# Channel sums of a fused convolution kernel, put off by one tick where a tick has neither a gate nor spectral work

## The chip, the cores and the metric

The kernel runs on one core of a Trainium2 chip. The metric is the device time of one execution in microseconds (us), as the median over several runs. Everything is fp32. The core has a matrix engine (PE, with a second queue PEld for its weight loads), a vector engine (DVE), a scalar engine (ACT), a general engine (POOL) and a queue engine (SP) that here only issues DMAs. PE writes to PSUM alone[...].

## The reference

Two residual layers on `x` of shape (8, 8, 512, 512), each behind a group norm. Cut to what the change touches:

```
# layer 0: x + spectral convolution of _gn(x), a few Fourier modes
# layer 1: x + f(_gn(x)), with f:
grid = drive
for _ in range(15):
    mapped = R * grid * (1.0 - grid)
    local = _conv(mapped, K_local, groups=8)           # 3x3, one filter a channel
    grid = (1 - BETA) * ((1 - EPS) * mapped + EPS * local) + BETA * drive
cml_out = clip(grid, 0.0001, 0.9999)
h = relu(_conv(x, Wp, bp))                             # 3x3, 8 -> 128 channels
nca_out = sigmoid(_conv(h, Wu, bu))                    # 1x1, 128 -> 8 channels
g = sigmoid(_conv(relu(_conv(concat(x, cml_out, nca_out), Wg1, bg1)), Wg2, bg2))
return g * cml_out + (1 - g) * nca_out
```

The 1x1 convolution from the 128 channels of `h` back to 8 is what the kernel calls a channel sum; it is the step that the change moves.

## The kernel before

The eight images ("elements") go through a hand-made schedule of *ticks*. A tick is one call of `work`, and the order in which `work` issues instructions is the order of every engine's queue: `keep_order` pins each engine to the order of the source. An element takes 45 ticks (56 to 415 in the kernel's own count for the eight together); before them stand a prologue with the first element's spectral layer and three ticks of rounds, after them 29 ticks of rounds and gates.

In a full tick the matrix engine gets, in this order:

1. **Three map sets.** A set is a slab of `m` (128 partitions, four rows of 514) that makes one of its 15 steps. `Slabs.convolve` (matmuls at L548) writes 48 products of 32x32 tiles into two of the four PSUM tiles; `settle` drains them with two DVE instructions of 128x1024 (L561), squares each half on ACT (L567), and `renew` swaps border rows with the neighbouring slab by four DMAs from POOL (L594, L595). `settle` is a generator: its first part (both L561, the first squaring) is issued right after the set's matmuls; the second squaring and `renew` come at the next `next(settled)`. For the third set of a tick that is inside the first round, behind the round's ACT instruction.
2. **Up to three rounds.** `Hidden.round` makes four rows of `h`: 12 matmuls at L749 into two PSUM tiles, drained half by ACT (L755) and half by DVE (L757). There are three `h` tiles.
3. **Channel sums** of those rounds. `Hidden.sums` groups the rounds by fours (round number // 4), so that a tick of three rounds has one group or two; `Hidden.point` makes four matmuls a round (L776) into one PSUM bank for each group. The first group of a four is copied to `y` by ACT (L783), a later one added by DVE (L785); when the four are complete ACT takes the sigmoid (L788), and the store of `y` (L791) is put into `rows_due`, which the next tick's `transfers()` empties.
4. **A gate**, where one is loaded (`Gate.conv` L833, `Gate.point` L850), and **spectral pieces** of the next element's layer 0, placed between and beside the channel sums.

In a tick with a gate the gate's matmuls stand between the last round and the sums, or between two groups.

The four PSUM tiles `pair0` to `pair3` are two *halves* of two tiles. `half()` hands them out in turn by the counter `used`: sets of a tick take A, B, A, rounds B, A, B; then the sums use the second tile of a half that the rounds have left (`first[1]`), after `used` has been raised once more:

```
first, second = halves[used[0] % 2], halves[(used[0] + 1) % 2]
if not others.spectral(WIDE, second):
    used[0] += 1
    first, second = second, first
groups = e.hidden.sums()
...
if len(groups) == 2:
    e.hidden.point(groups.pop(0), first[1][:, 0])
...
if groups:
    e.hidden.point(groups[0], first[1][:, 1])
```

The two groups of a tick lie in different banks of the same PSUM tile. In the built program the second group's first matmul nevertheless waits for the DVE addition (L785) that reads the first group's bank.

Map sets go in phases: four sets and then four sets and a tail, 15 steps each, set after set, so that a set comes again four or five places later.

Of the kernel before, what the change touches and what calls it, by code (L numbers as in the profile page):

```python
# [54 lines left out]
TICK = 3  # L55
WIDE, EARLY, FILL, LATE, LAST = "wide", "early", "fill", "late", "last"
# [63 lines left out]
def conv_layers(ctx: ExitStack, tc: tile.TileContext, a, out):  # L120
# [41 lines left out]


    put_off, now, rows_due = [], [0], []
    spare = deque()

    def later(ticks, work):
        put_off.append((now[0] + ticks, work))

    def tick(end=False):  # L170
        now[0] += 1
        due = [w for at, w in put_off if end or at <= now[0]]
        put_off[:] = [] if end else [(at, w) for at, w in put_off if at > now[0]]
        for work in due:
            work()
# [504 lines left out]
    class Phase:  # L680
# [25 lines left out]
        def squares(self, n):  # L706
            while self.squared < len(self.sets) and sets.room():
                if not self.ready(self.squared, 0, n + TICK):
                    break
                self.sets[self.squared].square()  # L710
                self.squared += 1
# [86 lines left out]
    class Gate:  # L798
# [59 lines left out]
        def finish(self):  # L858

            x1, o = (self.mix[: GR * C, q] for q in range(2))  # L860
            nc.vector.scalar_tensor_tensor(  # L861
                o, o, self.e.back[: GR * C, 0:1], x1, ALU.add, ALU.add
            )
            self.store()
# [71 lines left out]
    class Others:  # L936
# [52 lines left out]
        def busy(self):  # L989
            ahead = self.loaded or self.begun  # L990
            return self.before.gates or ahead or self.convolved or self.pointed

        def finish(self):
            while self.pointed:
                self.pointed.popleft().finish()
# [53 lines left out]
    def element(b):  # L1049
        e = Element(b)  # L1050
        phase(e.halves[0])
        phase(e.halves[1] + [e.tail])
        elements.append(e)
        return e

    e = element(0)
# [3 lines left out]
    others = Others()  # L1060
# [24 lines left out]
    halves = pairs[:2], pairs[2:]  # L1085
    used = [0]

    def work(steps, rounds, e, after, gates, transfers, squares=lambda: None):

        double = gates == 2 and not others.lag  # L1090

        def half():
            used[0] += 1
            return halves[used[0] % 2]

        settled = iter(())
        for n, (s, step) in enumerate(steps):
            ps = half()
            s.convolve(step, ps)
            next(settled, None)  # L1100
            if step == 1 and not s.driven:
                s.drive(1)
            settled = s.settle(step, ps)
            next(settled)
            others.finish()
            if gates == 2 and shared.most < 6:
                others.load(1)
                gates = 1
        if steps:
            others.finish()  # L1110
        transfers()
        if steps:
            had = len(others.loaded) + len(others.begun)
            others.load(gates, early=True)
            gates -= len(others.loaded) + len(others.begun) - had
        for _ in range(rounds):
            e.hidden.round(half(), after, settled)
            if spare:
                spare.popleft()()
        next(settled, None)  # L1120
        while spare:
            spare.popleft()()
        others.finish()
        squares()


        first, second = halves[used[0] % 2], halves[(used[0] + 1) % 2]
        if not others.spectral(WIDE, second):
            used[0] += 1
            first, second = second, first  # L1130
        groups = e.hidden.sums()
        gate = others.ready()
        if not gate:
            others.spectral(EARLY, [first[0][:, 0]])
        if len(groups) == 2:
            e.hidden.point(groups.pop(0), first[1][:, 0])
        two = False
        if gate:
            others.conv(first[0][:, 0])
            others.spectral(EARLY, [second[0][:, 0]])  # L1140
            two = others.ready(double)
            if two:
                others.conv(second[0][:, 0])
        if groups:
            e.hidden.point(groups[0], first[1][:, 1])
        others.spectral(FILL, [None])
        others.spectral(LATE, [second[1][:, 0]])
        others.point()
        others.spectral(LAST, [first[1][:, 0]])
        used[0] += two  # L1150
        others.load(gates)
        tick()
        squares()
# [26 lines left out]
    for b in range(B):  # L1180
        e = elements[b]
        after = element(b + 1) if b + 1 < B else None
        others.after = after
        done, rounds = e.hidden.n, ROUNDS if after else ROUNDS_LAST
        first, second = phases[2 * b : 2 * b + 2]
# [98 lines left out]
```

## Time and profile before

| | |
|---|---|
| median of 3 runs | 9116.31 us (9094.66, 9122.18, 9116.31) |
| profiled execution | 9110.93 us, span 9109.1 us, granted clock 0.993 |
| PE busy | 8724.3 us |
| DVE, ACT, POOL busy | 5843.4, 4097.1, 2674.7 us |
| L548 sets, L749 rounds, L776 sums on PE | 3665.0, 2771.8, 998.2 us |
| L833, L850 gates on PE | 951.3, 352.7 us |
| L561 on DVE, one of 128x1024 | 1218 ns |
| L785 on DVE, one of 128x512 | 686 ns (median) |
| L567 / L755 on ACT, one | 1056 / 1114 ns |

The busy time of PE counts matmuls that run beside each other in the array once; a matmul's own 0.6 us is its time through the pipeline, not its price. In lists of waits, "A <- B: total, times, longest" says for how long A's engine stood idle before A and that B's end let it go; "issue" means that nothing in the profile explains the idle time.

### The profile page before, as it was taken

The page shows a single profiled execution, that of the slowest core. Times are in us where ns is not written, and L with a number is a line of the kernel's source. Part 1 is how long each engine was busy: PE and PEld are TensorE (multiplying, and loading weights), DVE is VectorE, ACT ScalarE, POOL GpSimd, SP SyncE. Part 2 cuts the span into 40 slices and gives each one's busy share as a digit, 9 for nine tenths or more (in the row PEclk, how much of TensorE's full clock was granted, in tenths as well). Part 3 has the DMA queues.
Part 4 walks back from the last instruction along what each step waited for, and adds up shares of the span by engine and source line. Part 5 has one row for each costly group of instructions (what it writes and reads, how often), then busy time and mean ns, then how long its engine had stood idle before and what let it go on. Part 6 is the DMA issues. An engine that isn't in the chain of part 4 may idle for free. (4 is left out here: it accounts for less than half of the span.)

```text
span 9109.1 us, 334530 instructions
## 1 busy us (share of the span) xinstructions
PE 8724.3 (96%) x150992; PEld 4143.7 (45%) x150992; DVE 5843.4 (64%) x6304; ACT 4097.1 (45%) x4285; POOL 2674.7 (29%) x4010
## 2 busy tenths in 40 slices
PE   6999999999999999999999999999999999999999
PEld 2445544444444444444444444444444444444433
DVE  6665667656675566765677556775577655666654
ACT  2455445444444444444444444444444444444432
POOL 3222133232323323233232332323323233343323
PEclk9999999999999999999999999999999999999999
DMA  5241356745576555764557645575465754765488
GB/s 165 81 130 40 96 147 167 176 113 147 135 186 165 117 146 145 187 149 116 158 143 193 139 112 157 156 181 136 115 167 149 185 132 110 175 141 142 116 209 204
DMA packets 695970, 1327.26 MB, mean 146 GB/s; under 512 B 147680, under 2 KB 153184, under 8 KB 667056
## 3 DMA queue, kind: packets, MB, share of 16 engines
q1 hardware_dynamic: 587408, 1235.73, 52.9%
q0 software_dynamic: 104992, 69.33, 3.6%
q8 instruction: 1187, 19.45, 0.9%
q14 instruction: 239, 1.96, 0.1%
q10 hardware_dynamic: 2144, 0.80, 0.0%
HBM read 977.48 MB, written 270.61 MB: 137 GB/s over the span
## 5 line engine op out<-in xcount | busy, mean ns | idle before, releaser
L548 PE MATMUL pair<-m,band 32*32 32x512 f32 x103680 | 3665.0, 602 | 151.5 <-issue 125.4
L567 ACT ACTIVATE m<-m 128x1024 f32<-128x1024 f32 x2016 | 2129.1, 1056 | 2044.5 <-DVE m L561 1969.7
L548 PEld LDWEIGHTS pair<-m,band 32*32 32x32 f32 x103680 | 2148.4, 103 | 1601.5 <-issue 790.0
L749 PE MATMUL pair<-cols,w_p 32*128 32x511 f32 (+1 forms) x24576 | 2771.8, 596 | 20.2 <-DMA cols<-xn 12.1
L594 POOL DMA_DIRECT2D m<-m x1568 | 863.4, 551 | 4137.5 <-ACT m L567 4078.9
L749 PEld LDWEIGHTS pair<-cols,w_p 32*128 32x128 f32 x24576 | 1303.3, 185 | 1496.5 <-issue 1164.2
L561 DVE SCALAR_TENSOR_TENSOR m<-pair,dO 128x1024 f32<-128x1024 f32 x1152 | 1355.9, 1218 | 916.8 <-PE pair L548 796.2
L757 DVE TENSOR_SCALAR h<-pair,b_p 128x1024 f32<-128x1024 f32 x1024 | 1313.4, 1283 | 971.5 <-PE pair L749 953.2
L561 DVE SCALAR_TENSOR_TENSOR m<-pair,dE 128x1024 f32<-128x1024 f32 x1008 | 1186.7, 1218 | 845.5 <-PE pair L548 665.7
L755 ACT ACTIVATE h<-pair,b_p 128x1024 f32<-128x1024 f32 x1024 | 1140.1, 1114 | 1176.0 <-PE pair L749 1174.5
L776 PE MATMUL pair<-h,w_u 128*32 128x512 f32 x8192 | 998.2, 596 | 72.4 <-DVE y L785 47.3
L856 POOL TENSOR_TENSOR mix<-mix 96x512 f32<-96x512 f32 x344 | 437.0, 1275 | 1964.4 <-ACT mix L854 1964.3
L833 PE MATMUL pair<-gin,w_g 128*32 128x511 f32 (+1 forms) x8256 | 951.3, 597 | 25.9 <-DMA gin<-nca 15.1
L595 POOL DMA_DIRECT2D m<-m x1568 | 861.0, 549 | 53.8 <-issue 26.4
L833 PEld LDWEIGHTS pair<-gin,w_g 128*32 128x32 f32 x8256 | 252.7, 110 | 674.3 <-issue 602.7
L776 PEld LDWEIGHTS pair<-h,w_u 128*32 128x32 f32 x8192 | 246.4, 109 | 685.8 <-issue 519.4
L788 ACT ACTIVATE y<-y,b_u 128x512 f32<-128x512 f32 x256 | 184.9, 722 | 712.6 <-DVE y L785 712.5
L838 POOL TENSOR_TENSOR mix<-mix 96x512 f32<-96x512 f32 x344 | 444.1, 1294 | 142.4 <-DMA mix<-nca 81.6
L783 ACT COPY y<-pair 128x512 f32<-128x512 f32 x256 | 149.7, 585 | 644.7 <-PE pair L776 626.3
L843 DVE TENSOR_SCALAR mix<-pair,b_g 128x512 f32<-128x512 f32 x344 | 257.0, 747 | 204.2 <-PE pair L833 193.7
L850 PE MATMUL pair<-mix,w_g 128*32 128x512 f32 x2064 | 352.7, 598 | 36.7 <-DVE mix L843 33.1
L839 DVE SCALAR_TENSOR_TENSOR mix<-mix,back 96x512 f32<-96x512 f32 x344 | 311.3, 905 | 30.7 <-DMA mix<-nca 21.3
(96 smaller groups left out, 2612.0 us busy)
## 6 DMA issues: line engine op xcount, KB each, us to landing
gin<-xn SPq DMA_DIRECT2D x344, 384.0 KB
x<-in_x SPq DMA_DIRECT2D x120, 1024.0 KB
cols<-xn SPq DMA_DIRECT2D x240, 512.0 KB
gin<-cml SPq DMA_DIRECT2D x344, 320.0 KB
gin<-nca SPq DMA_DIRECT2D x344, 320.0 KB
dE<-xn SPq DMA_DIRECT2D x288, 256.0 KB
dO<-xn SPq DMA_DIRECT2D x288, 256.0 KB
mix<-xn SPq DMA_DIRECT2D x344, 192.0 KB
```

Source lines behind the costliest of these rows:

```text
L548: nc.tensor.matmul(ps[h // 2][32 * t : 32 * t + 32, h % 2], band[at, self.channel(step - 1, h, t), dx], m[at, t, dx : dx + N], start=(n == ...
L561: nc.vector.scalar_tensor_tensor(u[:, at], ps[q], FLOOR, d[:, at], ALU.max, ALU.add)
L567: nc.scalar.square(u[:, at], u[:, at])
L594: nc.gpsimd.dma_start(out=view(tb, rb, dims), in_=view(ta, ra, dims))
L595: nc.gpsimd.dma_start(out=view(ta, ra + s, dims), in_=view(tb, rb + s, dims))
L749: nc.tensor.matmul(ps[g // 2][:, g % 2, lo:hi], w_p[p, dx, i % 2], self.cols[p, i // 2, at : at + hi - lo], start=(n == 0), stop=(n == 2), ...
L755: nc.scalar.activation(h[:, :2], ps[0], AF.Relu, bias=b_p)
L757: nc.vector.tensor_scalar(h[:, 2:], ps[1], b_p, 0.0, ALU.add, ALU.max)
L776: nc.tensor.matmul(ps[32 * g : 32 * g + 32], w_u[:, r % 4], h[:, g], start=(r == hs[0][0]), stop=(r == hs[-1][0]), tile_position=(0, 32 * g),)
L833: nc.tensor.matmul(ps[32 * j : 32 * j + 32, lo:hi], gband[:, dx], gin[:, j, at : at + hi - lo], start=(n == 0), stop=(n == 2), tile_positi ...
L838: nc.gpsimd.tensor_tensor(d, d, ng, ALU.subtract)
L856: nc.gpsimd.tensor_tensor(d, d, mix[: GR * C, 2], ALU.mult)
```

## The change

A tick counts as *still* when it has three map sets and at least one round, loads no two gates at once, the next element has no spectral piece left (or there is no next element), and no gate is ready at its start. In a still tick the groups of channel sums are not issued; they go to the list `waiting`. The next tick, whatever it is, issues them after its three sets and its `transfers()`, before its rounds. They go into the second tile of the next half in turn, one bank for each group, and `used` is raised by one for them. In a still tick the turn at the end (`used[0] += 1` with the try of a wide spectral piece) is left out.

So around a still tick the halves go: sets A, B, A; the waiting sums B; rounds A, B, A; then the next tick's sets B, A, B. The first round now takes the half of the third set, where before it took that of the second.

```diff
@@ conv_layers
     put_off, now, rows_due = [], [0], []
+    waiting = []
     spare = deque()
@@ class Others
+        def idle(self):
+            return not (self.after and self.after.pieces) and not self.ready()
+
@@ work
+        still = len(steps) == TICK and rounds and not double and others.idle()
         settled = iter(())
         for n, (s, step) in enumerate(steps):
             ps = half()
...
         transfers()
+        for h, hs in waiting:
+            h.point(hs, halves[(used[0] + 1) % 2][1][:, hs[0][0] // 4 % 2])
+        if waiting:
+            used[0] += 1
+        waiting.clear()
         if steps:
             had = len(others.loaded) + len(others.begun)
...
         first, second = halves[used[0] % 2], halves[(used[0] + 1) % 2]
-        if not others.spectral(WIDE, second):
+        if not still and not others.spectral(WIDE, second):
             used[0] += 1
             first, second = second, first
         groups = e.hidden.sums()
         gate = others.ready()
+        if still:
+            waiting.extend((e.hidden, hs) for hs in groups)
+            groups = []
         if not gate:
             others.spectral(EARLY, [first[0][:, 0]])
```

Every instruction of the kernel before is still issued, as often as before; none is new. On POOL the order is the same instruction by instruction. On SP only the stores of `y` (L791) that belong to put-off sums move, one tick later. On DVE and ACT the additions, copies and sigmoids of those sums move from the end of a tick to the place behind the third set's L561 and first L567 of the next tick.

## Prediction

> **What bounds the kernel now.** I read the page first (engine shares, then the groups), then the list of PE's waits, then the timeline of PE and of DVE over three neighbouring ticks, and last the order of the built program's instructions with their waits.
>
> ```profile
> PE 8724.3 (96%) x150992; PEld 4143.7 (45%) x150992; DVE 5843.4 (64%) x6304; ACT 4097.1 (45%) x4285; POOL 2674.7 (29%) x4010
> L776 PE MATMUL pair<-h,w_u 128*32 128x512 f32 x8192 | 998.2, 596 | 72.4 <-DVE y L785 47.3
> ```
>
> PE is busy 96% of the span, so only its remaining 385 us (9109.1 - 8724.3) can be won, and part of that is the start. The change moves L776, before which PE idles 72.4 us in the whole run. PE's waits:
>
> ```profile
> PE pair L548 <- issue: 125.4, 77, 5.5
> PE pair L776 <- DVE y L785: 47.3, 35, 2.3
> ...
> PE pair L776 <- DVE h L757: 16.6, 29, 0.6
> ...
> PE pair L776 <- ACT h L755: 8.5, 19, 1.3
> ```
>
> The largest is idle time before map sets that no wait explains; the change doesn't address it. The three waits of L776 are what it can remove, where they fall into still ticks. Three such ticks of the first element, on PE and then on DVE:
>
> ```profile
> 653.54 9.76 PE L548 MATMUL pair<-m,band 32*32 32x512 f32 x288
> 663.23 8.00 PE L749 MATMUL pair<-cols,w_p 32*128 32x512 f32 x72
> 671.16 1.92 PE L776 MATMUL pair<-h,w_u 128*32 128x512 f32 x16
> 673.98 1.07 PE L776 MATMUL pair<-h,w_u 128*32 128x512 f32 x8 [0.90 <-DVE y L785]
> 674.98 9.76 PE L548 MATMUL pair<-m,band 32*32 32x512 f32 x288
> 684.66 8.00 PE L749 MATMUL pair<-cols,w_p 32*128 32x512 f32 x72
> 692.59 2.78 PE L776 MATMUL pair<-h,w_u 128*32 128x512 f32 x24
> 695.30 9.76 PE L548 MATMUL pair<-m,band 32*32 32x512 f32 x288
> 704.99 5.43 PE L749 MATMUL pair<-cols,w_p 32*128 32x512 f32 x48
> 710.35 1.06 PE L776 MATMUL pair<-h,w_u 128*32 128x512 f32 x8
> 711.68 1.23 PE L776 MATMUL pair<-h,w_u 128*32 128x512 f32 x8 [0.27 <-ACT h L755]
> ```
>
> ```profile
> 660.13 2.36 DVE L561 SCALAR_TENSOR_TENSOR m<-pair,dE 128x1024 f32<-128x1024 f32 x2 [0.76 <-PE pair L548]
> 663.30 2.35 DVE L561 SCALAR_TENSOR_TENSOR m<-pair,dE 128x1024 f32<-128x1024 f32 x2 [0.82 <-PE pair L548]
> 666.18 1.28 DVE L757 TENSOR_SCALAR h<-pair,b_p 128x1024 f32<-128x1024 f32 x1 [0.52 <-PE pair L749]
> ...
> 673.15 0.69 DVE L785 TENSOR_TENSOR y<-y,pair 128x512 f32<-128x512 f32 x1 [0.54 <-PE pair L776]
> ```
>
> Columns are start, duration, instruction, count, and idle time with its releaser. The reader is to see two things. A tick with three rounds and one group has no stall (692.59 follows on 684.66); one with two groups waits 0.90 us for the addition of the first group; one with two rounds waits 0.27 us for the drain of its last round. And DVE begins to drain the third set at 663.30, just as the rounds begin at 663.23: that is the moment into which the change puts the sums.
>
> **What the skill says.** "TensorE: Matmul & The Clock Gate", section "Part 3: Packing small matmuls", has matmuls start and end in strict program order, so that one that waits holds all behind it; the trace agrees (at 711.68 the sets behind are late too). "VectorE: DVE Perf Modes", section "The DRAIN you can't avoid", lets a DVE operation start only when the one before has left the pipe; here two L561 of 1.218 us take 2.35, so an addition behind them must wait for nearly all of both. "PSUM — Partial Sum Buffer", section "PSUM bank collisions raise a hardware error", forbids two engines one bank and quadrant at once but not two banks; the second group's wait for the first group's addition is thus the program's caution, not the chip's, and it stands in the built program of both kernels.
>
> **The change part by part.** Unrolled, the schedule has 60 still ticks: 28 in a row in the first element (ticks 73 to 100), four in each of the next six (118, 143 to 145, and so on) and eight in the last. Their sums are delivered as: 22 of one group with three rounds, 14 of one group with two rounds, 3 with one round, 21 of two groups (15 with two rounds and then one, 6 with one and then two).
>
> *Ideal pieces*, from the timeline: three sets 9.69 (653.54 to 663.23), three rounds 7.93 (684.66 to 692.59), a round less 2.57, three rounds' sums 2.71 (692.59 to 695.30), so 0.88 for one more. A stall-free tick is 20.32.
>
> *What is removed.* Two groups: the tick takes 21.44 (674.98 - 653.54), so 1.11 is lost; with one round in the first group 21.66 in the second element (2171.42 to 2193.08), 1.33 lost. Two rounds, one group: 17.53 against 20.32 - 2.57 - 0.88 = 16.87, 0.65 lost. One round: 1.2 us of idle time (tick 371, `L755`) and some 0.2 for the second half of its matmuls, 1.4. Three rounds, one group: 0. Sum: 15 x 1.11 + 6 x 1.33 + 13 x 0.65 + 3 x 1.4 = 37.3 us (in 13 of the 14; one shows none). That is the most the change can give.
>
> *What is put in its place.* Call the third set's end zero. The sums find their half drained (the second set's L561 end at 662.49, before 663.23) and start at once. DVE takes the third set's two L561 from 0.07 to 2.42 in any case. Two things now hang on them. First, the first round uses the third set's half, so its matmuls into the second tile wait until 2.42 + 0.14 = 2.56 (0.14 from 673.84, the end of an addition, to 673.98, the matmul it let go). Second, the first group's addition stands behind them on DVE and ends at 2.42 + 0.69 = 3.11, and the second group may start at 3.25.
> - Three rounds: sums end at 2.71, later than 2.56. No stall, as before: 0.
> - Two rounds: sums end at about 1.9; the stall is 0.65. As before: 0. One of the 14 goes to a tick without sets and wins 0.65.
> - One round: sums end at about 0.95, stall 1.6 against 1.4: 3 x 0.2 = +0.6.
> - Two then one: the second group is due at 1.83 and starts at 3.25: 1.42 against 1.11, 15 x 0.31 = +4.7.
> - One then two: due at 0.95, starts at 3.25: 2.30 against 1.33, 6 x 0.97 = +5.8.
>
> Direct sum: 0.6 - 0.65 + 4.7 + 5.8 = +10.4 us. The removed waits come back, a little longer, because the DVE is busy at the new place and idle at the old one (0.54 idle before the addition at 673.15).
>
> *Behind the waits.* On ACT the third set's second squaring stands behind the first round's L755, which comes up to 2.7 to 4.2 us later now; behind that squaring stand POOL's four border DMAs, and for them wait the sets one tick on. In the first element's still ticks these landed at least 5.2 us ahead of their matmuls, so that 1 to 2.5 us remain. Two ticks of the last element have less (0.04 and 1.46 us, ticks 372 and 390): +3 us, between 0 and +15 if landings slip. *Where a phase begins*, the DVE also scales a slab's drive (L540, 1.66 us) ahead of the third set's L561, which pushes both waits: ten such deliveries at an estimated 0.5 us, +5, between 0 and +10. *The sets after the rounds* need the half of the last but one round, drained during the last (1.28 of 2.57): nothing. *SP*: stores of `y` go one tick later; with two `y` tiles, the copy that reuses one comes some 11 us after the store is issued: nothing, or a few us where the queue is full. *POOL* order is unchanged. The 125.4 us of unexplained idle time may shift either way by an estimated 10.
>
> Sum: +18 us. Against the profiled execution 9110.9 + 18 = 9129; the median of the runs lies 5.4 above that execution, so I predict 9116 + 18 = **9134 us**.
>
> **The rivals.**
> - *The waits simply go.* If the program's wait for the addition could be met early, 37 us go: 9079. For it: the list of waits. Against it: DVE's order, in which the addition follows both L561 of the third set. 7%.
> - *Slower beyond doubt: the border rows become late.* The mechanism is ACT's queue: second squaring behind a later L755, four DMAs behind it, a set one tick on. It decides once landings take some 2 us longer than in this trace; then the 28 still ticks of the first element, and the last one's, lose 1 to 2 us each: some 35 us on top of the direct 10, 9160. For it: margins shrink from 5 to about 2 us, and the page gives 5.3 to 5.6 us as a median landing, not a bound. Against it: DMA traffic is low there (the DMA engines' mean busy share is 0.12 in windows over the three ticks). 25%.
> - *The forecast, with its small terms at their upper ends* (phase starts +10, late rows +8): 9116 + 10 + 18 = 9144, just over the line below. 20%.
> - *No effect that can be told*: a few us either way. It lies within the forecast's own range.
>
> **How the numbers follow.** About 0.3%, 27 us, is what a measurement of this kernel can tell from no change: 9089 to 9144. The forecast with the no-effect case has 48%, of which the forecast proper reaches from 9115 to 9144. The two slower cases have 45% and reach to 9165; the faster one 7%. So faster 0.07, same 0.48, slower 0.45. The range leaves out the faster case and the far end: 9107 to 9163.
>
> **What would show it.** Right: L776's wait for the addition (L785) stays, some 21 times in still ticks and now 1.4 to 2.3 us long; new waits of L749 for L561, under 1 us, where two rounds were put off; the total of PE's idle time up by 10 to 25 us; the triple of ticks above at about 59.6 instead of 59.3 us. Wrong: L776 without waits for L785 in the first element, or L548 waiting for `m<-m` more than a handful of times, or PE's unexplained idle time moved by more than 20 us.

## The result, and the profile after

| | before | after |
|---|---|---|
| median | 9109.53 us (4 runs, 9094.66 to 9122.18) | 9170.12 us (4 runs, 9159.59 to 9188.84) |
| ratio | | 1.0073, 95% interval 1.0061 to 1.0084 |
| profiled execution | 9110.93 us, span 9109.1 | 9160.4 us, span 9158.6 |

By the medians the kernel became 61 us slower (the interval of the ratio reaches from 56 to 77 us); 9134 had been predicted, with a range to 9163. The profiled execution of the kernel after was one of its two faster ones, so that the two traces lie 49.5 us apart, not 61. Line numbers after are higher by one (L549 for the sets' L548, L777 for the sums' L776, L784 for the copy into `y` at L783, L786 for the addition at L785, L792 for the store of `y` at L791). PE's waits in the kernel after, as idle time in us, times, and the longest:

```profile
PE pair L549 <- issue: 111.0, 76, 3.8
PE pair L777 <- DVE y L786: 61.8, 35, 2.4
PE pair L549 <- ACT y L784: 35.6, 6, 6.7
...
PE pair L777 <- DVE h L758: 16.6, 29, 0.6
...
PE pair L777 <- ACT h L756: 1.7, 7, 0.4
```

The wait for the addition grew by 14.5 us (47.3 before); the prediction had worked out 10.5. The third line is new: six times a map set waits for the copy of a sum into `y`. The triple of ticks in the first element whose ideal pieces the prediction used, on PE and on DVE:

```profile
678.59 1.93 PE L777 MATMUL pair<-h,w_u 128*32 128x512 f32 x16
681.66 1.06 PE L777 MATMUL pair<-h,w_u 128*32 128x512 f32 x8 [1.15 <-DVE y L786]
682.66 8.00 PE L750 MATMUL pair<-cols,w_p 32*128 32x512 f32 x72
690.59 9.76 PE L549 MATMUL pair<-m,band 32*32 32x512 f32 x288
700.27 2.78 PE L777 MATMUL pair<-h,w_u 128*32 128x512 f32 x24
702.99 5.43 PE L750 MATMUL pair<-cols,w_p 32*128 32x512 f32 x48
708.34 9.76 PE L549 MATMUL pair<-m,band 32*32 32x512 f32 x288
718.03 1.92 PE L777 MATMUL pair<-h,w_u 128*32 128x512 f32 x16
719.88 8.61 PE L750 MATMUL pair<-cols,w_p 32*128 32x512 f32 x72
```

```profile
678.66 2.36 DVE L562 SCALAR_TENSOR_TENSOR m<-pair,dO 128x1024 f32<-128x1024 f32 x2 [0.76 <-PE pair L549]
680.93 0.68 DVE L786 TENSOR_TENSOR y<-y,pair 128x512 f32<-128x512 f32 x1
```

Between sets and rounds the DVE is indeed at the third set's two drains when the sums arrive, and the addition follows them at 680.93 without a pause. The second group starts at 681.66, that is 3.07 us after the third set's end at 678.59 (3.25 predicted). Where two rounds were put off, the 0.65 us have moved into the rounds, which take 8.61 in place of 8.00 us and show no idle time before them. The triple takes 59.5 us (21.68 + 17.75 + 20.08) against 59.3 before: here the forecast holds.

The new wait stands in one tick at the end of each of six elements. At the end of the second element, from the timelines of PE, ACT and SP after:

```profile
2270.71 2.72 PE L777 MATMUL pair<-h,w_u 128*32 128x512 f32 x16
2273.36 3.83 PE L549 MATMUL pair<-m,band 32*32 32x512 f32 x100
2282.50 8.05 PE L549 MATMUL pair<-m,band 32*32 32x512 f32 x188 [5.31 <-ACT y L784]
```

```profile
2270.33 1.11 ACT L756 ACTIVATE h<-pair,b_p 128x1024 f32<-128x1024 f32 x1 [0.51 <-PE pair L750]
2281.86 0.58 ACT L784 COPY y<-pair 128x512 f32<-128x512 f32 x1 [10.41 <-DMA nca<-y]
```

```profile
2251.45 12.71 SPq L625 DMA_DIRECT2D cml<-m  x12
2264.28 8.27 SPq L792 DMA_DIRECT2D nca<-y  x1
```

To be read from the bottom: at the end of an element SP first issues twelve stores of `cml`, 12.71 us long; the store of `y` comes behind them and is itself 8.27 us in issue. ACT is free for the copy into `y` at 2271.44 and the sum that it copies ends on PE at 2273.43, but the copy reuses the tile that this store reads, and starts only at 2281.86. PE's next sets take the bank that the copy drains, and stop. Before, SP was no faster in the same tick:

```profile
2234.76 13.59 SPq L624 DMA_DIRECT2D cml<-m  x12
2248.45 8.70 SPq L791 DMA_DIRECT2D nca<-y  x1
```

but the `y` that the copy at 2255.98 replaced had been stored one tick earlier:

```profile
2208.97 8.16 SPq L624 DMA_DIRECT2D cml<-m  x9
2217.23 0.38 SPq L791 DMA_DIRECT2D nca<-y  x1
```

```profile
2255.98 0.59 ACT L783 COPY y<-pair 128x512 f32<-128x512 f32 x1 [1.59 <-PE pair L776]
```

The first tick of the next element (146 here) is the first that puts nothing off, because the spectral pieces of the element after it begin there. It delivers the sums of the tick before and its own. So its copy into `y` comes when it always came, while the store of the `y` before last, completed one delivery later, has slipped by a tick, behind the twelve. Before, the copies at these six places started 36 to 40 us after the issue of the store that frees their tile; after, the sums are ready 7.7 to 10.1 us behind that issue, and the tile is free only after 17.4 to 18.2 us. The seventh end shows the same by contrast: its store is as slow (8.34 us), but tick 371 puts its own sums off too, the copy comes 24.5 us behind the store, and nothing waits.

The six ticks whose sets stop (102, 147, 192, 237, 282, 327) took 148.5 us before and 193.7 after by the trace: 45.2 of the 49.5 us between the two spans. Of these 45.2 us, 31.9 are idle time of PE in these ticks (17.7 before, 49.6 after). The other 13.3 are busy time, with the same number of matmuls. The record of the granted clock accounts for most of it. Tick 147 before, then after, and then the stop and the time behind it; PEclk, the third number from the end, is the share of its full clock that PE was granted:

```profile
2255.86:2279.32 23.46, 21.12 (x451) 11.78 (x449) 19.19 (x21) 11.16 (x13) 5.41 (x10) 1.00 0.67 233
```

```profile
2273.36:2304.75 31.39, 23.79 (x450) 12.65 (x448) 19.18 (x21) 10.93 (x13) 5.41 (x10) 0.95 0.52 180
```

```profile
2277.19:2282.50 5.31, 0.00 (x1) 0.01 (x1) 1.99 (x2) 0.64 (x2) 0.00 (x0) 0.98 0.62 233
2282.50:2285.70 3.20, 3.20 (x64) 1.21 (x65) 0.00 (x0) 1.84 (x2) 1.07 (x3) 0.50 0.10 39
```

In each of the six ticks a stretch of 3.4 or 6.8 us at half clock begins 2.6 to 5.2 us after PE has stopped. PE was busy at half clock for 29.1 us in the six ticks, 4.3 before; half of the difference, 12.4 us, is an estimate of what that cost. In `after_store` and `after_early` below, where the stop is gone, it is 4.4 and 0.8 us.

In the run of still ticks of the first element, the trace shows 477.5 and 482.0 us from tick 76 through 99, which is +4.5. From the first still tick (73) to the tick that delivers the last of their sums (101), it is 585.2 and 585.9 us.

### The profile page after: what moved, and what is told of

Its sections match the earlier page's. It is cut to its first block, busy times and chain, and to the rows that moved or that the text cites. A ratio compares the mean times of both kernels' runs of the same rounds, so it can differ in the third digit from the quotient of the medians.

```text
span 9158.6 us, 334510 instructions
## 1 busy us (share of the span) xinstructions
PE 8741.7 (95%) x150992; PEld 4140.8 (45%) x150992; DVE 5839.2 (64%) x6304; ACT 4093.5 (45%) x4285; POOL 2673.5 (29%) x4010
## 5 line engine op out<-in xcount | busy, mean ns | idle before, releaser
L549 PE MATMUL pair<-m,band 32*32 32x512 f32 x103680 | 3674.0, 603 | 177.6 <-issue 111.0
L549 PEld LDWEIGHTS pair<-m,band 32*32 32x32 f32 x103680 | 2137.5, 103 | 1640.3 <-issue 780.9
L777 PE MATMUL pair<-h,w_u 128*32 128x512 f32 x8192 | 1001.1, 600 | 83.5 <-DVE y L786 61.8
L777 PEld LDWEIGHTS pair<-h,w_u 128*32 128x32 f32 x8192 | 242.9, 110 | 704.3 <-issue 496.5
L784 ACT COPY y<-pair 128x512 f32<-128x512 f32 x256 | 149.5, 584 | 710.4 <-PE pair L777 629.8
```

What stands on the lines that cost most here:

```text
L549: nc.tensor.matmul(ps[h // 2][32 * t : 32 * t + 32, h % 2], band[at, self.channel(step - 1, h, t), dx], m[at, t, dx : dx + N], start=(n == ...
L777: nc.tensor.matmul(ps[32 * g : 32 * g + 32], w_u[:, r % 4], h[:, g], start=(r == hs[0][0]), stop=(r == hs[-1][0]), tile_position=(0, 32 * g),)
```

## The experiments

Theory A: the late store of `y`. Theory B: the sums' new place, behind busy DVE and ACT. Theory C, the prediction's slower rival: late border rows. The kernel before was run again beside each set: 9103.75 us for the first, 9104.14 for the second, 9104.62 for the third. Differences below are against the run beside. The kernel after was not run again with them, so that what "comes back" is counted from the 61 us of the first comparison.

**A third `y` tile** (`after_y3`), and the same on the kernel before as its control (`before_y3`). To make room, the two tables of sines share one tile.

```diff
-                self.y = wk.tile([P, N], F32, tag="y", name="y", bufs=2)
+                self.y = wk.tile([P, N], F32, tag="y", name="y", bufs=3)
...
-    e2 = cp.tile([P, N], F32, name="e2")
+    e2 = e1
...
-                p = slice(32 * j, 32 * j + 8)
+                r = 32 * (1 + j % 3)
+                p = slice(r, r + 8)
```

> The kernel after with three y tiles in place of two (and, to make room, the two tables of sines share one tile). Theory A, the store of y: at the end of an element the copy into y waits for the store that frees its tile, and this is most of the loss. Then the 35.6 us of map sets waiting for the copy (L784) vanish and 35 to 48 us come back: 9120 to 9135 us, 0.1 to 0.3% over before. Theory B, the place of the sums: DVE and ACT are busy behind the third set, and all still ticks pay. Then nothing comes back: 9160 to 9175. Theory C, late border rows: as B.

> The kernel before with three y tiles and the shared table of sines: the control for the run beside it. All theories: within 0.1% of the kernel before, about 9110 us, since no copy into y waited for a store in its map phase.

Measured: 9140.35 us, ratio to before 1.0039 (1.0024 to 1.0054), and for the control 9127.85, 1.0026 (1.0017 to 1.0035). The control missed: the shared table costs 24 us by itself, for a reason that stays open, and so the run itself lies 5 us over its range. Against the control 12 us of the 61 are left. The sets' wait for the copy is gone from the list of waits of `after_y3`, and its six ticks take 155.0 us (153.0 in the control). The store behind the twelve is as slow as before (8.19 us in tick 146), but the copy that reuses its tile now comes 37 us behind it. This is Theory A, with a remainder about as large as the forecast's own terms.

**Still ticks of the first element alone, or of all others** (`after_first`, `after_others`).

```diff
-        still = len(steps) == TICK and rounds and not double and others.idle()
+        still = len(steps) == TICK and rounds and not double and others.idle() and now[0] < 99
```

The other has `now[0] > 100` at the end.

> The kernel after with still ticks in the first element alone, 26 of the 60, the last of them two ticks before the element ends. Theory A: no loss to speak of, -5 to +8 us against before, since sums that are put off there leave no two deliveries of different ticks at an element's end. Theory B: its share of the loss, 26/60 of 60 us, +26. Theory C: +15 to +40, as these are the shortest ticks.

> The kernel after with the still ticks of the first element left as before: 32 of the 60 remain, among them those at the ends of all elements but the first. Theory A: the loss stays but for the first element's end, 60 less some 10: 9150 to 9165 us. Theories B and C, by the count of ticks: about half, 9125 to 9140.

Measured: 9107.14 us, 1.0005 (0.9996 to 1.0014), and 9159.47 us, 1.0061 (1.0048 to 1.0073). So 26 still ticks in a row cost 3 us, which can't be told from nothing, and 32 at the ends of phases and elements cost 55: the loss doesn't go by the number of ticks, against B as the main cause, nor is it in the shortest ticks, against C. The six ticks take 151.0 and 187.6 us. In `after_others` the wait has one place less:

```profile
PE pair L549 <- ACT y L784: 30.9, 5, 7.2
```

Five elements end behind a still tick there, and the trace gives those five ticks 30.93 to 33.91 us. The sixth, tick 102, where nothing was put off, takes 23.46 (24.59 in the kernel before).

**The store of `y` earlier.** `after_store` and its control `before_store` empty `rows_due` at the end of every tick, ahead of the stores of `cml`; `after_early` does so only for the stores that put-off sums completed.

```diff
         others.load(gates)
+        while rows_due:
+            rows_due.pop()()
         tick()
```

```diff
         waiting.clear()
+        early = len(rows_due)
...
         others.load(gates)
+        for _ in range(early):
+            rows_due.pop(0)()
         tick()
```

> The kernel after with the stores of y issued at the end of the tick, ahead of the stores of cml, in place of behind the next tick's map sets. Theory A: the tile is free earlier, 30 to 48 us come back, 9120 to 9140. Theories B and C: nothing, 9160 to 9175.

> The kernel before with the stores of y at the end of the tick: the control for the run of the kernel after with that edit. If the store matters only where sums are put off, within 0.15% of before, 9095 to 9117; if the early store is good by itself, 20 us or more faster.

> The kernel after in which only stores of y completed by put-off sums are issued early, at the end of the tick that delivers them; all other stores stay as before. If the late store is the cause, and the 14 us that the early store cost the kernel before come from ticks in which the sum has only just been issued, the loss falls to the 0 to 12 us left by the waits: 9103 to 9118. If early stores cost 14 us wherever they stand: 9118 to 9130.

Measured: `after_store` 9118.86 us, 1.0016 (1.0010 to 1.0023); `before_store` 9118.27, 1.0019 (1.0012 to 1.0026); `after_early` 9120.38, 1.0016 (1.0010 to 1.0023). The loss falls from 61 us to 15 (the control loses 14 too) and to 16: issuing the stores of `y` earlier on SP's queue, and nothing else, gives back some 45. The sets' wait for the copy is gone from both lists of waits, and the six ticks take 150.1 and 149.9 us. In `after_store` SP issues the store in 0.41 us, and the twelve come behind it:

```profile
2240.49 0.41 SPq L792 DMA_DIRECT2D nca<-y  x1
2240.99 13.32 SPq L625 DMA_DIRECT2D cml<-m  x12
2254.63 8.69 SPq L186 DMA_DIRECT2D x<-in_x  x2
```

The control was a miss again, slower and not level. As `after_early` kept all other stores where they were and lies 16 us over before all the same, the 14 us of the control and the last 15 us here need not be the same thing; which part of these 15 is the sums' place and which the early store isn't settled. The second range of `after_early` (early stores cost 14 us wherever they stand) holds the result; that reason was not tested further.

**Two PSUM tiles for the two groups**: `after_tiles`, on the kernel before `before_tiles`, and together with the early stores `after_store_tiles` and `after_early_tiles`.

```diff
-            h.point(hs, halves[(used[0] + 1) % 2][1][:, hs[0][0] // 4 % 2])
+            h.point(hs, halves[(used[0] + 1) % 2][hs[0][0] // 4 % 2][:, 0])
```

```diff
         if groups:
-            e.hidden.point(groups[0], first[1][:, 1])
+            free = not gate and not (others.after and others.after.pieces)
+            e.hidden.point(groups[0], first[0][:, 1] if free else first[1][:, 1])
```

> The kernel after with the two waiting groups in the two PSUM tiles of their half in place of two banks of one tile, so that the program no longer makes the second group wait for the addition of the first. If the wait for the addition (L786) is what the new place costs, 15 x 1.42 + 6 x 2.30 = 35 us come back: 9125 to 9140. If it is only a name for the DVE's drain of the third set, which the first round waits for as well, less than 10 us come back: 9155 to 9175.

> The kernel before with the second group of a tick without gate and spectral pieces in the other tile of its half, nothing put off. If the waits in the still ticks are the program's caution about one PSUM tile, 15 x 1.11 + 6 x 1.33 = 25 us go: 9075 to 9090 us. If DVE is needed by the second group anyway (the drain of the last round), under 8 us.

> The kernel after with both edits: the stores of y at the end of the tick, and the two groups in two tiles. If the losses add up, 60 less 47 for the stores (as measured alone) less 35 for the additions: 9075 to 9090 us, 0.2 to 0.3% under before. If the additions' wait hides another wait, 9110 to 9125.

> The same with the two groups in two tiles. If the parts add up: the run beside it less 35 to 45 us, 9060 to 9080, so faster than the kernel before by 0.3 to 0.5%, and level with or under the kernel before with two tiles (9080).

| kernel | median us | ratio to before (95%) |
|---|---|---|
| after_tiles | 9125.67 | 1.0028 (1.0018 to 1.0039) |
| before_tiles | 9080.06 | 0.9976 (0.9968 to 0.9984) |
| after_store_tiles | 9085.21 | 0.9984 (0.9976 to 0.9992) |
| after_early_tiles | 9090.54 | 0.9983 (0.9976 to 0.9990) |

`after_tiles` loses 22 us where the kernel after lost 61: 39 come back, where 35 had been expected. Its waits, and those of `before_tiles`:

```profile
PE pair L777 <- DVE y L786: 26.6, 14, 2.3
PE pair L549 <- ACT y L784: 24.7, 6, 6.3
```

```profile
PE pair L776 <- DVE y L785: 24.2, 12, 2.3
```

Of 61.8 us of waiting for the addition 35.2 are gone, in 21 places: as many as there are deliveries of two groups. The wait for the copy is lower too, 24.7 in place of 35.6. So the wait for the addition was a price of its own. It also shows what the wait hung on: the two groups lay in different banks (halves of 128x512 of a PSUM tile) before and after the edit, and only the tile is another. On the kernel before a like edit brings 24 us (25 expected) without anything being put off; 23 of the 35 waits are gone. `before_tiles` is faster than both kernels and has the lowest median of the versions tried; `after_store_tiles`, 5 us over it, can't be told from it. `after_early_tiles` was expected at 9060 to 9080 us, under `before_tiles`, and isn't.

## Why the prediction was wrong

*What is removed*, 37.3 us at most: the parts that were tried hold. The two-group waits come to 24.6 in its sum, and `before_tiles` brought 24. That the chip itself would have let the second group write to the other bank of the same tile is argued in the prediction; no run here tried it.

*What is put in its place*: held, to a tenth or two in single ticks. A tick that gets two groups takes 21.68 us (20.32 + 1.42 = 21.74 predicted), one that gets three rounds' sums 17.75 with two rounds of its own, no stall, and one that gets two 20.08 with 0.6 in the rounds. The reading that one DVE operation starts only when the one before is through holds to 0.1 us: the addition starts at 680.93, the drains' record ends at 681.02. The waits for L786 grew by 14.5 us, where 10.5 had been worked out for the two-group deliveries. With the store out of the way 12 us of loss remained against the control (`after_y3`), 1 us against the control (`after_store`), or 16 us (`after_early`, which has no control); the whole forecast was 18, and how much of it was there is open.

*Behind the waits, border rows*: the rival C was not it. Sets waiting for `m<-m` came to 2.5 us, four times, in the kernel after (2.1 before), and the first element, where the margins were counted, lost 3 us in `after_first`. Tick 372, which it singled out, did grow, from 17.81 us to 24.41, but not through border rows: sets waited 1.63 us for `m<-m` there before and 0.50 after. After, this tick makes the sums of two ticks, and the granted clock in it was 0.86 (1.00 before).

*Behind the waits, SP*: this is the step that failed. It read: "stores of `y` go one tick later; with two `y` tiles, the copy that reuses one comes some 11 us after the store is issued: nothing, or a few us where the queue is full." The mechanism was named and priced at nothing; the runs put 45 us there. The distance was about right: in the six places the sums were ready 7.7 to 10.1 us after the store's issue began. What was wrong is how long such a store holds its tile. A store that SP issues at once can be done by then: one tick earlier the copy came 8.24 us behind the store that frees its tile, and did not wait for it:

```profile
2234.80 0.36 SPq L792 DMA_DIRECT2D nca<-y  x1
```

```profile
2243.03 0.59 ACT L784 COPY y<-pair 128x512 f32<-128x512 f32 x1 [0.43 <-PE pair L777]
```

The store at 2264.28 stood behind the twelve stores of `cml` and held its tile for 17.6 us (2264.28 to 2281.86). The change brings the two together only in the first tick behind the still ones, which delivers twice; there it cuts the distance from 38.75 us to 9.2. The lines for it were in the trace before: SP's 13.59 us for the twelve, and the 8.70 us of that one store. The forecast also had no term for the clock, which added to the cost of each stop.

Of the signs that it named, L777's waits for the addition stayed and the triple came to 59.5 us. PE's idle time grew by 32.1 us (384.8 to 416.9), where 10 to 25 had been said; the wait for the copy alone is 35.6, and it was not among the signs.

The chances gave a slower kernel 45%, but the rival of that size stood on border rows: that the measured time lies near its 9160 us is luck.

## What to carry to other kernels

When work is put off, follow the buffers that it fills through to the DMA that empties them, in the tick where the putting off *ends*: there the late delivery and the next one on time meet, and here two buffers were one too few, because that DMA stood behind twelve others. Ask how long the DMA takes in that place, not in the mean. A wait that a view names may be removable where it stands: here it came from two groups that shared a PSUM tile in different banks, and another tile for the second brought 24 us, where moving the work lost 61. Measure a control of every edit that comes along to make an experiment possible: two of these controls were slower by 14 and 24 us.

## What the runs showed of the hardware

One DMA instruction on SP, a store of 256 KB, took 0.44 us to issue in the median of 237 (kernel before). In all seven places right behind twelve stores of `cml` it took 8.0 to 9.5 us before and 5.7 to 9.1 after, and nowhere else more than 2.2. Right behind nine stores of `cml` it took 0.38 (at 2217.23). In `after_store`, where the store stands ahead of the twelve, the next DMA behind them pays: six times a load of `x`, 6.7 to 8.5 us, and once the next store of `y`, 7.3. The price is that of the place behind the twelve, whatever comes there. Why twelve and not nine, no run shows.

A stop of PE cost more than its idle time: in the six ticks PE was idle for 31.9 us more than before, and the ticks were 45.2 us longer. Each stop was followed by 3.4 or 6.8 us at half the clock, part of it in the matmuls behind the stop, an estimated 12 us in all.
